# Transpositions of the normed x in the bank of the sums, in turn with the down products

## The chip, the cores and the metric

The kernel runs on one core of one Trainium2 chip. The metric is device time in microseconds of one execution: the median of several runs, here 661.32 us (three runs: 663.54, 661.32 and 660.82). Beside these stands one execution taken by the hardware profiler, from which all durations come.

## The reference

One transformer block in fp32 with the layer norm behind each residual sum, for x of shape 4 x 512 x 512 (batch, token, feature). The attention has 16 query heads of 32 and a single key and value head, with rotary positions; the feed-forward part has 1408 hidden units and ternary weights.

```python
q = rotary((x @ Wq + bq) heads); k = rotary(x @ Wk + bk); v = x @ Wv + bv
attn = softmax(q @ k.T / sqrt(32)); ctx = attn @ v
x = layernorm(x + ctx @ Wo + bo)
quantize(w) = clip(round(w / (mean(abs(w)) + 1e-8)), -1, 1)
hidden = sigmoid(x @ quantize(w1).T) * (x @ quantize(w2).T)
x = layernorm(x + hidden @ quantize(w3).T)
```

## The kernel before, in words

**Work and order.** The attention is cut into 64 steps (`steps`, L791): four batches b, four groups c of four heads, four tiles t of 128 keys. Step by step, `scores` (L414) writes the scores of one key tile for four heads into two double banks (PE, four products `ps` with the keys, then four that add minus the row maximum), ScalarE exponentiates them (`es`), and one step later `weigh` (L455) multiplies with v into `acc`. Each step also looks for the row maxima of a step seven ahead: `maximum` (L379) multiplies q and k again in the other orientation, one chunk of 128 queries at a time, and VectorE reduces each chunk (`maxima<-pmax`). The main loop (L865 on) issues chunk 0, then chunks 1 and 2 together, then chunk 3.

Everything else is filling between these pieces. `Fill` (L742) holds two lists of generators, `urgent` with the output projection of a batch (`project_out`, L588) and `gens` with the input projection and then `feed_forward` (L622), and takes from them in turn, one piece each, up to the microseconds due. A piece that yields 0 passes its turn to the other list. So while step n of batch b + 1 is computed, the output projection of batch b and the feed-forward part of batch b - 1 come to lie in between.

`project_out` ends with the part that is changed: for each of the four token tiles, four PE transpositions (`transpose`, L85) of the normed x into one bank `pt`, then `split` (L577): ScalarE copies the bank to a rounded y0, VectorE subtracts y0 from the bank to give y1 (`y<-pt,y`). Both halves, of all four tiles, are operands of the next batch's gate and up products (`gu`). `s.transposed` counts the tiles done.

`feed_forward` works in groups of hidden tiles. After the last group come the last down products: `po` for token tiles 0 and 1 together (twelve products), then for tile 2, then for tile 3 (six each). After each, VectorE adds half of `po` to x (`xt<-po,xt`, L700) and takes the statistics of the norm (`stats`, L560: `st`, `mv`). The loop at L681 holds these pieces back until the next batch has transposed enough tiles: two tiles before the first piece, three before the second, four before the third; after the last step (`now == len(steps)`) three, four and four.

**Banks.** The eight banks of the accumulator memory are split so: `ps_sc` has two double banks for scores and for maxima; `ps_acc` has one bank `acc` and one bank `den`; `ps_mm` has two single banks, taken in turn by every other product (`bank`, L226; in the tail every second one comes from `ps_sc`). `den` holds the sums of the exponentials in batch 0 (`count`, L464) and is the "bank of the sums" of the title. From batch 1 on POOL adds up the exponentials, and `den` serves for maxima: always that of chunk 0, and, once the last batch has been projected (`batches[-1].done == NC`), that of chunk 3 too (L385). A bank is free again when the engine that reads it has finished; whoever wants it next waits.

**What sets the order.** Each engine, and the queue of DMAs on SP, executes its instructions in the order in which the program issues them (`pin`, L67, forbids a reordering). PE, VectorE and ScalarE thus wait in line behind whatever stands ahead.

Of the kernel before, what the change touches and what calls it, by code (L numbers as in the profile page):

```python
# [10 lines left out]
F32 = mybir.dt.float32  # L11
# [9 lines left out]
P = 128  # L21
# [7 lines left out]
def postln_block(  # L29
# [16 lines left out]
    B, T, D = x.shape  # L46
    NC = D // P
    NT = T // P
    NF = wf.shape[1]
# [14 lines left out]
    ps_acc = ctx.enter_context(tc.tile_pool(name="ps_acc", bufs=1, space=PSUM))  # L64
# [14 lines left out]
    def mm(out, lhsT, rhs, start, stop):  # L79
        pin(nc.tensor.matmul(out, lhsT=lhsT, rhs=rhs, start=start, stop=stop))  # L80
# [36 lines left out]
    batches = [Batch() for _ in range(B)]  # L117

    chunks = iter([(b, c) for b in range(B) for c in range(NC)])
# [102 lines left out]

    swap = [(i + HALF) % HD for i in range(HD)]
    others = cycle((False, True))

    def bank(name):  # L226

        if now == len(steps) and next(others):
            return ps_sc.tile([P, 2, T], F32, tag="sc", name=name)[:, 0, :]
        return ps_mm.tile([P, T], F32, tag="mm", name=name)  # L230
# [133 lines left out]
    def room_for_maxima(b, c):  # L364

        return maxima[c % 2][:, 0 : NG * NT].rearrange("p (i t) -> p i t", t=NT)
# [12 lines left out]
    def maximum(b, c, i, chunks, q):  # L379


        s = batches[b]
        if i == 0 and chunks[0] == 0:
            s.mx[c] = room_for_maxima(b, c)
        if len(chunks) == 1 and (chunks[0] == 0 or batches[-1].done == NC):  # L385
            ps = ps_acc.tile([P, 1, T], F32, tag="den", name="pmax")
        else:
            ps = ps_sc.tile([P, 2, T], F32, tag="sc", name="pmax")
        ps = ps[:, 0 : len(chunks), :]
        for n, t in enumerate(chunks):  # L390
            mm(ps[:, n, :], q[:, ts(t, P)], s.kr, True, True)
        dve.tensor_reduce(s.mx[c][:, i, chunks[0] : chunks[-1] + 1], ps, AX.X, ALU.max)
# [195 lines left out]
    def project_out(b):  # L588

        s = batches[b]  # L590
        s.transposed = 0
        mv = small.tile([P, NT, 2], F32, tag="mv", name="mv")
        for t in range(NT):
            po = ps_mm.tile([P, D], F32, tag="mm", name="po")
            for c in range(NC):
                mm(po, s.ctxT[c][:, ts(t, P)], wo_sb[:, c, :], c == 0, c == NC - 1)
                if c == 1:
                    yield -1.8
            dve.tensor_tensor(s.x[t], s.x[t], po, ALU.add)
            stats(s.x[t], mv, t)  # L600
            if t == NT - 1:
                late.append((slot + 1, layernorm(s.x, mv)))
                ready = slot + 5
                s.projected = True
            yield 1.8

        while slot < ready or (b and not batches[b - 1].y_done):
            yield 0
        s.w = [load_weight(m, 0) for m in range(2)] + [load_weight(0, 1)]
        s.y = [work.tile([P, NC, T], F32R, tag=f"y{i}", name=f"y{i}", bufs=1) for i in range(2)]  # L610
        s.y_done = False
        for t in range(NT):
            pt = bank("pt").rearrange("p (c m) -> p c m", m=P)
            for c in range(NC):
                transpose(pt[:, c, :], s.x[t][:, ts(c, P)], ident)
            y = [half[:, :, ts(t, P)] for half in s.y]
            split(*y, pt)
            s.transposed = t + 1
            yield 0.9
        fill.add(feed_forward(b))  # L620

    def feed_forward(b):  # L622

        s = batches[b]
        mv = small.tile([P, NT, 2], F32, tag="mv2", name="mv2")
        after = [(m, f) for f in range(NF) for m in range(2)][3:]

        short = NF % 4 if b + 1 == B else 0
        ends = sorted({0, NF, *range(short, NF, 4)})
        parts = [range(*pair) for pair in zip(ends, ends[1:])]  # L630
        w3 = [[] for _ in parts]
        th = {}

        def product(k, m):
            w = s.w.pop(0).rearrange("p (c m) -> p c m", c=NC)
            if after:
                s.w.append(load_weight(*after.pop(0)))
            if len(w3[k]) < len(parts[k]):
                w3[k].append(load_weight(2, parts[k][len(w3[k])]))
            g = bank("gu")  # L640
            for c in range(NC):
                for i, part in enumerate(s.y):
                    mm(g, w[:, c, :], part[:, c, :], c == 0 and i == 0, c == NC - 1 and i == 1)
            return g

        def gate(k, f):

            th[f] = work.tile([P, T], F32, tag="th", name="th")
            act.activation(th[f], product(k, 0), AF.Tanh, scale=0.5)
            if b + 1 == B and f + 1 == NF:  # L650

                root = small.tile([P, 1], F32, tag="row", name="root")
                act.activation(root, eps_t, AF.Sqrt)

        for k, fs in enumerate(parts):
            h = []
            for f in fs:
                if f not in th:
                    gate(k, f)
                    yield 1.9  # L660
                up = product(k, 1)
                hw = work.tile([P, T], F32, tag="hw", name="hw")
                dve.scalar_tensor_tensor(hw, th[f], 1.0, up, ALU.add, ALU.mult)
                s.y_done = f == NF - 1
                h.append([hp.tile([P, T], F32R, tag="h", name=f"h{i}") for i in range(2)])

                if f == fs[-1]:
                    act.copy(h[-1][0], hw)
                yield 1.9
                if f < fs[-1]:  # L670
                    act.copy(h[-1][0], hw)
                dve.tensor_tensor(h[-1][1], hw, h[-1][0].bitcast(F32), ALU.subtract)
            if fs[-1] + 1 < NF:
                gate(k + 1, fs[-1] + 1)
                yield 1.9

            ahead = NT // 2 if fs[-1] + 1 == NF else 1
            for some in [range(ahead)] + [(t,) for t in range(ahead, NT)]:


                while fs[-1] + 1 == NF and b + 1 < B and 0 <= batches[b + 1].transposed <= min(  # L681
                    some[-1] + (now == len(steps)), NT - 1
                ):
                    yield 0
                pos = {t: bank("po") for t in some}
                last = len(fs) - 1
                early = [(t, n) for t in some for n in range(last)]

                put = len(early) - 1 if b + 1 == B and len(some) > 1 else len(early)
                for t, n in early[:put] + [(some[0], last)] + early[put:] + [(t, last) for t in some[1:]]:  # L690
                    for i in range(2):
                        mm(
                            pos[t],
                            h[n][i][:, ts(t, P)],
                            w3[k][n],
                            n == 0 and i == 0,
                            n == last and i == 1,
                        )
                for t in some:
                    dve.scalar_tensor_tensor(s.x[t], pos[t], 0.5, s.x[t], ALU.mult, ALU.add)  # L700
                    if fs[-1] + 1 < NF:
                        continue
                    stats(s.x[t], mv, t)
                    if b + 1 == B:
                        for done in range(max(t - 1, 0), t):
                            norm = layernorm(s.x[done : done + 1], mv[:, done : done + 1, :], True)
                            next(norm)
                            if t + 1 == NT:
                                end = last_scale(mv[:, t, :])
                            for _ in norm:  # L710
                                pass
                            late.append((slot + 1, store(b, done)))
                        if t + 1 == NT:
                            last_norm(s.x[t], *end)
                    elif t == NT - 1:
                        late.append((slot + 1, layernorm(s.x, mv)))
                yield 0.24 * 2 * len(fs) * len(some)
        if b + 1 < B:
            for t in range(NT):
                late.append((slot + 6, store(b, t)))  # L720
# [70 lines left out]
    steps = [(b, c, t) for b in range(B) for c in range(NC) for t in range(NT)]  # L791
# [6 lines left out]
    now = -1  # L798
# [66 lines left out]
    for n, (b, c, t) in enumerate(steps):  # L865
        now = n
# [46 lines left out]
    now = len(steps)  # L913
# [68 lines left out]
```

## Time and profile before

| | |
|---|---|
| median of the runs | 661.32 us |
| the profiled execution | 659.87 us, of which 658.1 us is its span |
| PE busy | 635.4 us, 3194 products |
| VectorE (DVE) busy | 440.3 us |
| ScalarE (ACT) busy | 282.6 us |
| GpSimd (POOL) busy | 327.4 us |
| granted PE clock, mean | 0.997 |
| 64 transpositions `pt<-ident,xt` | 272 ns each (median), from 227.0 to 587.6 us of the span |
| 16 copies `y<-pt` on ACT / 16 subtractions `y<-pt,y` on DVE | 586 ns / 681 ns each (median) |

The transpositions of batch 0 lie at 227 to 233 us of the span, those of batch 1 at 360 to 373, those of batch 2 at 495 to 509, and those of batch 3 after the last step, up to 588.

A row of the profile's groups reads: line and engine, operation, tile written <- tiles read (buffer numbers left out), shape, number of instructions | busy us, mean ns of one | idle us of the engine just before them, and which instruction ended most of that idle time. Nearly all PE work has line L80 and nearly all VectorE and ScalarE work L75, as small helpers issue them; so tiles are what to go by. A row of the timeline reads: start in the span, duration, engine, operation, and in brackets the idle time before it and what ended it. Neighbouring instructions of one kind are merged into one row, which then lasts from the first start to the last end. Ends of PE's products are modelled, and PE issues the next before the end of the last.

### The profile page before, as it was taken

Reading aid. Unit: us, or ns where it says so; the run is one execution under the profiler, and the core shown is the slowest. Engines: PE = TensorE matmul, PEld = TensorE weight load, DVE = VectorE, ACT = ScalarE, POOL = GpSimd, SP = SyncE. Lnnn points to the kernel's source line nnn. Section 1 sums busy time; section 2 is a strip of 40 time slices with the busy share of each in tenths; the row PEclk is TensorE's granted clock in tenths of the full one; section 3 lists DMA queues with packets and bytes.
Section 4 is the critical chain, followed back from the end, with each engine's and each line's share of the span. In section 5 each row is a group of like instructions: output and inputs, shape, how many; then the busy total and the mean of one; then the engine's idle time right before and its main releaser. Section 6 shows DMA issues by size and latency. Waiting matters only on the chain.

```text
span 658.1 us, 9358 instructions
## 1 busy us (share of the span) xinstructions
PE 635.4 (97%) x3194; PEld 357.2 (54%) x3194; DVE 440.3 (67%) x629; ACT 282.6 (43%) x441; POOL 327.4 (50%) x416
## 2 busy tenths in 40 slices
PE   8999999999999999999999899999998999999995
PEld 5233333443333356665555566655555685778884
DVE  3987765787998977676666867667536544364335
ACT  2474656564454645333244354333454521234213
POOL 2434344545998766467666275576575703202000
PEclk9999999999999999999999999999999999999998
DMA  8946669788676286464132457541131473237531
GB/s 265 316 164 209 204 194 273 230 254 259 171 238 205 89 250 190 136 191 147 46 106 77 117 163 219 158 143 44 55 116 52 145 236 120 81 112 229 175 109 64
DMA packets 60671, 107.78 MB, mean 164 GB/s; under 512 B 14592, under 2 KB 15360, under 8 KB 60624
## 3 DMA queue, kind: packets, MB, share of 16 engines
q1 hardware_dynamic: 51984, 80.57, 40.2%
q0 software_dynamic: 7920, 25.96, 12.3%
q10 hardware_dynamic: 720, 0.66, 0.4%
q8 instruction: 25, 0.41, 0.3%
q14 instruction: 22, 0.18, 0.1%
HBM read 84.06 MB, written 23.10 MB: 163 GB/s over the span
## 4 chain that ended last, share of the span: by engine, by line
PE 85%; DVE 9%; ACT 4%; issue 2%; POOL 0%; DVEq 0%; ACTq 0%; POOLq 0%
PE gu L80 24%; PE po L80 19%; PE ps L80 13%; PE pmax L80 9%; PE acc L80 7%; PE pq L80 7%; DVE maxima L75 3%; ACT es L75 2%; PE den L80 2%; PE pk L80 2%; DVE part L75 1%; DVE xt L75 1%; DVE y L75 1%; DVE st L75 1%; PE warm L80 1%
## 5 line engine op out<-in xcount | busy, mean ns | idle before, releaser
L75 DVE TENSOR_REDUCE maxima<-pmax 128x1 f32<-128x512 f32 (+1 forms) x169 | 157.8, 955 | 69.9 <-PE pmax L80 69.7
L75 ACT ACTIVATE es<-ps 128x1024 f32<-128x1024 f32 x128 | 124.2, 1021 | 117.6 <-PE ps L80 116.7
L80 PE MATMUL gu<-y,wg 128*128 128x512 f32 x704 | 171.6, 393 | 0.1
L80 PEld LDWEIGHTS gu<-y,wg 128*128 128x128 f32 x704 | 131.7, 188 | 33.7 <-issue 4.9
L75 POOL TENSOR_TENSOR total<-total,es 128x512 f32<-128x512 f32 x96 | 125.2, 1336 | 38.5 <-ACT es L75 38.3
L80 PE MATMUL po<-wd,h 128*128 128x512 f32 x352 | 86.5, 394 | 3.3 <-DVE y L75 2.9
L75 POOL TENSOR_TENSOR total<-es 128x512 f32<-128x512 f32 x48 | 60.9, 1302 | 52.5 <-ACT es L75 52.5
L80 PE MATMUL pmax<-kr,qr 128*128 128x512 f32 x192 | 74.7, 452 | 3.2 <-DVE maxima L75 1.0
L80 PEld LDWEIGHTS po<-wd,h 128*128 128x128 f32 x352 | 65.1, 188 | 20.8 <-DVE y L75 4.6
L75 ACT CAST h<-hw 128x512 fp32r<-128x512 f32 x44 | 27.3, 620 | 103.0 <-DVE hw L75 103.0
L80 PE MATMUL acc<-es,v 128*32 128x512 f32 x512 | 68.2, 605 | 0.0
L80 PEld LDWEIGHTS pmax<-kr,qr 128*128 128x128 f32 x192 | 34.6, 188 | 55.9 <-issue 17.0
L75 DVE SCALAR_TENSOR_TENSOR hw<-th,gu 128x512 f32<-128x512 f32 x44 | 30.2, 686 | 44.3 <-PE gu L80 43.1
L80 PE MATMUL po<-wo_sb,ctxT 128*128 128x512 f32 x128 | 58.8, 592 | 0.0
L75 DVE TENSOR_TENSOR h<-hw,h 128x512 fp32r<-128x512 f32 x44 | 44.2, 1005 | 21.7 <-ACT h L75 21.4
L80 PE MATMUL ps<-negm,ones_r 2*128 2x512 f32 x256 | 58.7, 788 | 0.0
L75 DVE SCALAR_TENSOR_TENSOR xt<-po,xt 128x512 f32<-128x512 f32 x48 | 32.8, 684 | 37.0 <-PE po L80 37.0
L80 PE MATMUL ps<-qT,kT 32*128 32x512 f32 x384 | 56.3, 640 | 0.0
L75 POOL DMA_DIRECT2D raw<-in_wf x66 | 36.0, 548 | 38.1 <-DMA w<-raw 27.2
L80 PE MATMUL pq<-xT,wq_sb 128*128 128x512 f32 x112 | 53.1, 602 | 0.9 <-ACT v L75 0.9
L75 ACT ACTIVATE th<-gu 128x512 f32<-128x512 f32 x44 | 26.3, 597 | 49.9 <-PE gu L80 49.8
L80 PEld LDWEIGHTS po<-wo_sb,ctxT 128*128 128x128 f32 x128 | 24.1, 189 | 21.2 <-issue 19.2
(99 smaller groups left out, 640.2 us busy)
## 6 DMA issues: line engine op xcount, KB each, us to landing
wg<-w SPq DMA_DIRECT2D x88, 256.0 KB
raw<-in_wf POOLq DMA_DIRECT2D x66, 256.0 KB, 4.6
qr<-qp SPq DMA_DIRECT2D x96, 128.0 KB
wd<-w SPq DMA_DIRECT2D x44, 256.0 KB
w<-raw POOLq DMA_DIRECT2D x33, 256.0 KB, 4.6
qp<-q SPq DMA_DIRECT2D x48, 128.0 KB
rden<-flat SPq DMA_DIRECT2D x64, 64.0 KB
xt<-in_x SPq DMA_DIRECT2D x16, 256.0 KB
```

Source lines behind the costliest of these rows:

```text
L75: return lambda *args, **kw: pin(getattr(self.engine, name)(*args, **kw))
L80: pin(nc.tensor.matmul(out, lhsT=lhsT, rhs=rhs, start=start, stop=stop))
```

## The change

Three things, all for the transpositions of batches 0, 1 and 2, and none after the last step:

- Their bank. Of batch 0, tiles 0 and 3 go into `den` and tiles 1 and 2 into `ps_mm`; of batches 1 and 2, tiles 0, 1 and 3 go into `den` and tile 2 into `ps_mm`.
- The maximum of chunk 3. In a step in which `den` has been given to a transposition (`turned`), it goes into a scores' bank in place of `den`.
- The turns. The first down piece (token tiles 0 and 1) waits for one transposed tile in place of two; the second and third wait as before. With the turns that `Fill` takes, the order for batches 1 and 2 is pt0, po0 and po1, pt1, pt2, po2, pt3, po3, where it was pt0, pt1, po0 and po1, pt2, po2, pt3, po3. For batch 0 there are no down products in between.

No instruction is added or taken away; the order on SP and POOL is unchanged, and so is that of VectorE and ScalarE for batch 0.

```diff
--- before.py
+++ after.py
@@ -222,6 +222,7 @@
 
     swap = [(i + HALF) % HD for i in range(HD)]
     others = cycle((False, True))
+    turned = [-1]
 
     def bank(name):
 
@@ -382,7 +383,7 @@
         s = batches[b]
         if i == 0 and chunks[0] == 0:
             s.mx[c] = room_for_maxima(b, c)
-        if len(chunks) == 1 and (chunks[0] == 0 or batches[-1].done == NC):
+        if len(chunks) == 1 and (chunks[0] == 0 or batches[-1].done == NC and turned[0] < now):
             ps = ps_acc.tile([P, 1, T], F32, tag="den", name="pmax")
         else:
             ps = ps_sc.tile([P, 2, T], F32, tag="sc", name="pmax")
@@ -610,7 +611,13 @@
         s.y = [work.tile([P, NC, T], F32R, tag=f"y{i}", name=f"y{i}", bufs=1) for i in range(2)]
         s.y_done = False
         for t in range(NT):
-            pt = bank("pt").rearrange("p (c m) -> p c m", m=P)
+            if now == len(steps) or (t in (1, 2) if b == 0 else t == 2):
+                pt = bank("pt")
+            else:
+
+                pt = ps_acc.tile([P, D], F32, tag="den", name="pt")
+                turned[0] = now
+            pt = pt.rearrange("p (c m) -> p c m", m=P)
             for c in range(NC):
                 transpose(pt[:, c, :], s.x[t][:, ts(c, P)], ident)
             y = [half[:, :, ts(t, P)] for half in s.y]
@@ -678,8 +685,8 @@
             for some in [range(ahead)] + [(t,) for t in range(ahead, NT)]:
 
 
-                while fs[-1] + 1 == NF and b + 1 < B and 0 <= batches[b + 1].transposed <= min(
-                    some[-1] + (now == len(steps)), NT - 1
+                while fs[-1] + 1 == NF and b + 1 < B and 0 <= batches[b + 1].transposed <= (
+                    min(some[-1] + 1, NT - 1) if now == len(steps) else some[-1] if len(some) == 1 else 0
                 ):
                     yield 0
                 pos = {t: bank("po") for t in some}
```

## The prediction

> **What bounds the kernel.** I read the page first: the busy shares, then the chain that ended last.
>
> ```profile
> span 658.1 us, 9358 instructions
> ...
> PE 635.4 (97%) x3194; PEld 357.2 (54%) x3194; DVE 440.3 (67%) x629; ACT 282.6 (43%) x441; POOL 327.4 (50%) x416
> ...
> PE 85%; DVE 9%; ACT 4%; issue 2%; POOL 0%; DVEq 0%; ACTq 0%; POOLq 0%
> ```
>
> TensorE (PE) is busy in 97% of the span, and 85% of the final chain is its work. Only about 22.7 us of PE idle exist in all, so the change can win only what is idle at the places it touches, and every microsecond of new PE idle is added to the time in full, because nothing later has slack to give it back. So the next view is PE's groups with the idle time just before them (instructions, busy us, mean ns | idle us and what ended it):
>
> ```profile
> L80 PE MATMUL po<-wd,h 128*128 128x512 f32 x352 | 86.5, 394 | 3.3 <-DVE y L75 2.9 <-DVE xt L75 0.3
> ...
> L86 PE MATMUL pt<-ident,xt 128*128 128x128 f32 x64 | 9.6, 278 | 3.7 <-DVE y L75 2.2 <-DVE q L75 1.1 <-DVE xt L75 0.3
> ```
>
> The transpositions (pt) and the down products (po) wait 7.0 us together, nearly all for a bank of `ps_mm` that VectorE (DVE) still reads. Where: the busy times by stretch (length, then PE, PEld, DVE, ACT, POOL busy, clock) of the three places where a batch's transpositions run inside the attention of a later batch:
>
> ```profile
> 226.00:235.00 9.00, 6.69 (x48) 3.02 (x40) 8.72 (x15) 5.32 (x8) 8.98 (x9) 1.00 0.82 243
> 358.00:374.00 16.00, 13.60 (x80) 8.26 (x78) 13.55 (x22) 5.39 (x9) 5.83 (x5) 1.00 0.46 133
> 495.00:511.00 16.00, 14.14 (x86) 8.06 (x86) 10.99 (x18) 6.54 (x9) 9.65 (x8) 1.00 0.17 52
> ```
>
> PE idles 2.31, 2.40 and 1.86 us there: 6.57 us is all that can be won (1.0%). The same lines warn: at the first two places DVE is busy 8.72 of 9 and 13.55 of 16 us. DVE's order is fixed, so whatever PE is made to wait for stands in a nearly full queue. The fourth batch's transpositions (from 575 us on) run after the last step, where the change keeps bank and order; they cost nothing new.
>
> **The change, place by place.** It adds and removes no instruction, and the queues of SP (DMA) and POOL keep their order. What changes is which bank each transposition has, hence what it waits for, and at the second and third place the order "pt0 pt1 | po0 po1 | pt2" becomes "pt0 | po0 po1 | pt1 pt2". From the built order of the changed kernel I took the instruction that each wait is for, and laid it on the times of this trace. Four durations recur, in us: `pt` x4 to the next PE instruction 0.36; one `po` product 0.25; scores' first `ps` to the first `acc` 1.30 (second pair of `ps` to `acc` 1.02); a single-chunk maximum on DVE 0.68.
>
> *First place.*
>
> ```profile
> 229.06 0.68 DVE L75 TENSOR_REDUCE maxima<-pmax 128x1 f32<-128x512 f32 x1
> 229.20 0.66 PE L86 MATMUL pt<-ident,xt 128*128 128x128 f32 x4 [1.13 <-DVE q L75]
> 232.13 0.66 PE L86 MATMUL pt<-ident,xt 128*128 128x128 f32 x4 [1.07 <-DVE y L75]
> 232.71 1.14 PE L80 MATMUL ps<-qT,kT 32*128 32x512 f32 x8
> ```
>
> Now pt0 runs at 227.01 in a free `ps_mm` bank. In the sums' bank (`den`) it must wait until DVE has reduced the maximum of chunk 0 that lies there, and DVE, still rotating q, starts that at 229.06: pt0 starts at 229.79. Queued behind pt0 on PE are two maxima products, the other transpositions and the scores; ScalarE (ACT) copies y at 230.5 (0.58), so DVE's first y starts at 231.10 instead of 229.7. The two later waits of pt (1.13 and 1.07) do go. But the maximum of chunk 3 has moved from `den` to the scores' banks, so the second pair of `ps` must wait for its reduction. DVE needs 3.01 from the first y to that reduction's end: 234.1. `acc` follows 1.02 later at 235.2; it was at 234.01. **+1.2 us.** Below: all 2.31 of idle go; above: pt0's whole delay of 2.78 (227.01 to 229.79) stays. I take the replay, as DVE is the full queue.
>
> *Second place.*
>
> ```profile
> 363.61 0.67 DVE L75 TENSOR_REDUCE maxima<-pmax 128x1 f32<-128x512 f32 x1
> 365.44 0.69 DVE L75 SCALAR_TENSOR_TENSOR xt<-po,xt 128x512 f32<-128x512 f32 x1 [1.15 <-PE po L80]
> 365.79 1.14 PE L80 MATMUL ps<-qT,kT 32*128 32x512 f32 x8
> 367.09 1.06 PE L80 MATMUL acc<-es,v 128*32 128x512 f32 x8
> 368.62 1.82 DVE L75 TENSOR_REDUCE maxima<-pmax 128x1 f32<-128x512 f32 x2
> 372.22 0.66 PE L86 MATMUL pt<-ident,xt 128*128 128x128 f32 x4 [1.11 <-DVE y L75]
> 373.63 0.66 DVE L75 TENSOR_REDUCE maxima<-pmax 128x1 f32<-128x512 f32 x1
> ```
>
> Here the down products no longer wait 0.98 and 0.31 for y; they wait for the last hidden chunk instead (DVE's h ends at 363.08, PE is there at 362.5), and PE reaches the scores at 364.25, 1.5 earlier. Then it stops. The product of chunk 3 now stands behind po0 and po1, so its reduction stands on DVE behind both additions into x and their statistics; and it lies in a scores' bank, so the second `ps` pair waits for it. DVE starts the first addition at 363.6 and needs 3.18 from there to the next reduction (365.44 to 368.62): the maximum runs 366.8 to 367.5, `ps` at 367.5, `acc` at 368.5 instead of 367.09: +1.4. Next step: maxima product of chunk 0 at 369.5, its reduction (PE to DVE 0.54, then 0.69) to 370.76, and only then pt1, as it is in `den`: 1.0 of PE idle. Then y1 (DVE 372.1), double maximum, the partial sum (1.23), y2, the third addition at 375.6 and, 1.54 behind that (372.09 to 373.63 in the trace), the reduction of chunk 3: 377.2 to 377.85. Again the second `ps` pair waits for it, where now it needs only ACT: `acc` at 378.9 instead of 374.11. **+4.8 us** together; ACT's exponentials, POOL's totals and later DVE work follow PE and have waits of their own to fill. SP's next load of heads waits for the moved product, 3 us later than now; behind it in SP's queue stands only the store of the partial sum, for which SP now waits 10.0 us. Below: −2.40 (all idle goes, the reductions are in time); above: the 3.18 of queue paid whole in both steps, +6.4.
>
> *Third place.*
>
> ```profile
> 501.12 2.11 PE L80 MATMUL po<-wd,h 128*128 128x512 f32 x8 [1.18 <-DVE y L75]
> 503.56 0.66 PE L86 MATMUL pt<-ident,xt 128*128 128x128 f32 x4 [0.33 <-DVE xt L75]
> 508.89 1.66 PE L80 MATMUL po<-wd,h 128*128 128x512 f32 x6 [0.35 <-DVE xt L75]
> ```
>
> All maxima are done, so `den` is really free. po0 and po1 start at 498.35 in banks freed long ago; pt2 is ready when the first addition ends (501.8); scores at 502.4 instead of 504.15; po3 needs y2 (505.4) and finds it done; the gate product ends up waiting 0.3 for the last y (508.6) and starts in effect at 508.4 instead of 510.41. **−2.0 us** (idle is counted from modelled matmul ends, so 1.86 of idle is 2.3 of lost issue). Below −2.3, above 0.
>
> **Sum.** +1.2 + 4.8 − 2.0 = +4.0. The profiled execution took 659.87 us (1.77 around its span): 663.9. The median of the runs shown is 661.32, which gives 665.3. I forecast **665.0**.
>
> **A rule that would make it worse.** In this trace PE never idles longer than 1.5 us, and the granted clock in all three stretches is 1.00; my replay has PE idle some 3.0 us (364.5 to 367.5) and 3.1 us (374.8 to 377.9). The Trainium skill, "TensorE: Matmul & The Clock Gate", section "What's actually happening", says that about 3.4 us of idle halve PE's clock until about 3.4 us of work have passed. No run here shows it yet; were a gap to count, an estimate from that page is 1.7 us more per gap, 668.4 for two.
>
> **Rivals.** *Faster:* the banks were the whole matter. Place: the scores' second `ps` pair at the second place. It decides from the point where the chunk-3 reductions end before PE gets there (by 364.5 and 374.7). Then that place gives up to −2.4, with the other two −3.2; if the first place's maximum also came in time, −6.57. Middle: 656.5. For it: the idle rows name exactly the banks that are changed. Against: the reductions would have to run 3 us earlier in a fixed queue. *No change:* only one of the two chunk-3 waits binds, because the trace's modelled PE ends hide some slack; 4.0 − 3.3 (the second wait's share, 4.8 − 1.4, nearly) = +0.7: 662.0. For it: DVE idles 1.15 just ahead of the first addition. *Worse:* both queues count whole (+6.4 at the second place) and the first place pays 2.78: +7.2, 668.5.
>
> **How the numbers follow.** Within 0.5% is 658.0 to 664.6, about what a measurement of this kernel can tell from no change. Forecast's case (+2.5 to +6, 663.8 to 667.3): 0.64, of which 0.09 falls within 0.5%; no change 0.22; worse 0.06; faster 0.08. So faster 0.08, same 0.31, slower 0.61. The range takes in the forecast's case and no change, and half a microsecond of run spread: 660.5 to 668.0.
>
> **What would show it.** Right: at about 227 us PE idle of some 2.5 before pt, ended by DVE maxima; about 365 and 376 us PE idle of 2.5 to 3 each before `ps`, ended by DVE maxima, a group that has no idle now; near 500 no idle before po. Wrong: no idle before `ps`, or the reductions of chunk 3 ahead of the additions on DVE. If `ps` waits but the time does not grow, my claim that PE has no slack later is wrong.

## The result and the profile after

The changed kernel takes 667.81 us (median of 6 runs, 667.32 to 670.95), the kernel before in the same runs 662.23 us (6 runs, 660.73 to 664.94). The ratio is 1.0089, with a 95% interval of 1.0069 to 1.0109: about 5.9 us slower, where I had forecast 3.7 us. The profiled execution took 667.70 us. The page of the changed kernel, read as before:

```profile
span 665.9 us, 9357 instructions
...
PE 641.1 (96%) x3194; PEld 360.4 (54%) x3194; DVE 439.0 (66%) x629; ACT 282.7 (42%) x441; POOL 328.0 (49%) x416
...
PEclk9999999999999999999999799999999999999998
...
PE 83%; DVE 8%; ACT 3%; DMA 2%; issue 2%; POOL 1%; SPq 0%; DVEq 0%; ACTq 0%; POOLq 0%
```

The span is 7.8 us longer with the same number of products. Idle time of PE grew by only 2.1 us (24.8 against 22.7); the other 5.7 us are *busy* time, 641.1 against 635.4. A part of that is only a way of counting: as the ends of products are modelled, the last products before a stop count as busy while PE already waits (at 367.45 below, four score products take 1.13 us; before the change eight took 1.14). For another part the clock strip names the reason: one slice of 40, at about 370 us, has a 7. The changed kernel's groups with the idle time before them:

```profile
L80 PE MATMUL po<-wd,h 128*128 128x512 f32 x352 | 87.0, 396 | 1.1 <-DVE h L75 0.7 <-DVE y L75 0.5
L80 PE MATMUL ps<-qT,kT 32*128 32x512 f32 x384 | 59.7, 640 | 3.6 <-DVE maxima L75 3.5
L86 PE MATMUL pt<-ident,xt 128*128 128x128 f32 x64 | 10.1, 294 | 3.4 <-DVE maxima L75 3.4
```

The down products' wait fell from 3.3 to 1.1 us, as the new banks were to do. The transpositions wait as long as before, but now for a maximum in `den`. And the scores, which had no such wait, lose 3.6 us to the maxima of DVE.

**First place** of the changed kernel, timeline:

```profile
229.74 0.68 DVE L75 TENSOR_REDUCE maxima<-pmax 128x1 f32<-128x512 f32 x1
230.48 0.66 PE L86 MATMUL pt<-ident,xt 128*128 128x128 f32 x4 [2.57 <-DVE maxima L75]
233.67 1.90 PE L80 MATMUL ps<-qT,kT 32*128 32x512 f32 x6 [0.47 <-DVE maxima L75]
236.16 1.06 PE L80 MATMUL acc<-es,v 128*32 128x512 f32 x8
```

The 2.57 before pt0 is the wait that I foresaw (2.5), and `acc` starts at 236.16 instead of 234.01 (0.73 of this is a lag from the start of the kernel, see below).

**Second place**, timeline (the changed kernel arrives here 3.15 us late):

```profile
366.87 0.69 DVE L75 SCALAR_TENSOR_TENSOR xt<-po,xt 128x512 f32<-128x512 f32 x1 [0.59 <-PE po L80]
367.45 1.13 PE L80 MATMUL ps<-qT,kT 32*128 32x512 f32 x4
369.94 0.66 DVE L75 TENSOR_REDUCE maxima<-pmax 128x1 f32<-128x512 f32 x1
370.65 0.70 PE L80 MATMUL ps<-qT,kT 32*128 32x512 f32 x2 [2.07 <-DVE maxima L75]
371.95 1.64 PE L80 MATMUL acc<-es,v 128*32 128x512 f32 x8
375.10 1.12 PE L86 MATMUL pt<-ident,xt 128*128 128x128 f32 x4 [0.78 <-DVE maxima L75]
377.57 2.35 PE L80 MATMUL po<-wd,h 128*128 128x512 f32 x6
381.88 0.66 DVE L75 TENSOR_REDUCE maxima<-pmax 128x1 f32<-128x512 f32 x1
382.60 0.70 PE L80 MATMUL ps<-qT,kT 32*128 32x512 f32 x2 [0.94 <-DVE maxima L75]
383.89 1.07 PE L80 MATMUL acc<-es,v 128*32 128x512 f32 x8
```

The first pair of scores (four rows of the trace) runs at 367.45, and then PE has nothing that it may do until DVE has reduced chunk 3 behind the two additions: the maximum ends at 370.60, the second pair starts at 370.65. The same comes back at 382.60. Now compare durations: eight `acc` take 1.64 us at 371.95 and 1.07 at 383.89; four `pt` take 1.12, where they took 0.66; six `po` take 2.35 (1.64 in a place with full clock). So for a part of the time between the two waits PE works at half its speed. The stretches, each 3.41 us (length, then PE, PEld, DVE, ACT, POOL busy, clock):

```profile
368.89:372.30 3.41, 1.65 (x12) 0.65 (x16) 1.64 (x4) 0.40 (x1) 0.00 (x0) 1.00 0.93 200
372.30:375.71 3.41, 2.63 (x12) 0.90 (x5) 0.69 (x1) 2.02 (x3) 0.00 (x0) 0.50 0.04 11
375.71:379.13 3.42, 3.42 (x13) 2.83 (x12) 2.26 (x3) 1.18 (x2) 0.00 (x0) 0.50 0.02 5
```

In the first, PE is busy for 1.65 of 3.41 us; in the next two the granted clock is 0.50. In the trace's record of the clock this is the only drop between the first microseconds and PE's last product: at 372.3 us, for 6.83 us. The trace of before has none in that time. (An estimate: PE's 6.05 us of work at half clock would take 3.0 us less at full clock, which is about half of the 5.7 us of added busy time.)

**Third place**, timeline:

```profile
508.15 3.14 PE L80 MATMUL po<-wd,h 128*128 128x512 f32 x12
511.13 1.14 PE L86 MATMUL pt<-ident,xt 128*128 128x128 f32 x8
512.19 1.14 PE L80 MATMUL ps<-qT,kT 32*128 32x512 f32 x8
```

No idle time stands before any of them: down products, transpositions and scores follow each other.

To see where the 7.8 us of span come from, I took the 512 `acc` products of both traces in their order, and noted how much later each starts:

| part of the span | growth of the lag, us |
|---|---|
| start, up to 52 us, where nothing is changed | +0.73 |
| first place (234 us), and a wait for weights in the next step | +1.41, +0.17 |
| a wait for weights at 300 us (0.58 before `gu`) | +0.84 |
| second place, first and second step (367 and 374 us) | +1.71, +4.92 |
| third place | −1.75, −0.22 |

The three places alone give 1.41 + 6.63 − 1.97 = +6.1 us, which agrees with the measured ratio (5.9). The rows at the start and at 300 us belong to this pair of executions: such shifts of 0.5 to 1 us come at several points in traces of several kernels below.

### The profile page after: what moved, and what is told of

Same layout as the page of the kernel before. It is cut to its first block, busy times and chain, and to the rows that moved or that the text cites. A ratio compares the mean times of both kernels' runs of the same rounds, so it can differ in the third digit from the quotient of the medians.

```text
span 665.9 us, 9357 instructions
## 1 busy us (share of the span) xinstructions
PE 641.1 (96%) x3194; PEld 360.4 (54%) x3194; DVE 439.0 (66%) x629; ACT 282.7 (42%) x441; POOL 328.0 (49%) x416
## 4 chain that ended last, share of the span: by engine, by line
PE 83%; DVE 8%; ACT 3%; DMA 2%; issue 2%; POOL 1%; SPq 0%; DVEq 0%; ACTq 0%; POOLq 0%
PE gu L80 23%; PE po L80 19%; PE ps L80 12%; PE pmax L80 9%; PE acc L80 7%; PE pq L80 7%; DVE maxima L75 3%; PE den L80 2%; ACT es L75 2%; PE pk L80 2%; DMA wg<-w 2%; DVE st L75 1%; DVE xt L75 1%; DVE part L75 1%; PE warm L80 1%
## 5 line engine op out<-in xcount | busy, mean ns | idle before, releaser
L80 PE MATMUL ps<-qT,kT 32*128 32x512 f32 x384 | 59.7, 640 | 3.6 <-DVE maxima L75 3.5
L80 PE MATMUL ps<-negm,ones_r 2*128 2x512 f32 x256 | 60.2, 780 | 0.0
L75 DVE TENSOR_TENSOR h<-hw,h 128x512 fp32r<-128x512 f32 x44 | 42.7, 971 | 21.8 <-ACT h L75 21.4
```

Source lines behind the costliest of these rows:

```text
L75: return lambda *args, **kw: pin(getattr(self.engine, name)(*args, **kw))
```

## Experiments

After the result I held this, called A in the expectations: the second place loses because chunk 3's maximum lies in a scores' bank while its reduction stands on DVE behind the additions that the new turns put ahead of it; a part of the loss is the halved clock that follows the stop; the third place gains for free. Rivals: the turns alone do it, the banks alone do it, or the clock is only a companion and costs nothing. Edits are against the changed kernel unless said otherwise.

**One place at a time.** `first_only`, `second_only` and `third_only` make the change for one batch (0, 1, 2) and leave the two others as before:

```diff
-            if now == len(steps) or (t in (1, 2) if b == 0 else t == 2):
+            if now == len(steps) or b not in (1,) or (t in (1, 2) if b == 0 else t == 2):
...
-                    ... else some[-1] if len(some) == 1 else 0
+                    ... else some[-1] if len(some) == 1 or b + 1 not in (1,) else 0
```

*First place alone.* 

> Only batch 0's transpositions get the new banks (and chunk 3 of that step moves); batches 1 and 2 keep the old banks and turns. My replay gave +1.2 us for this place and the two traces put it at +1.4, so: 1.2 to 1.6 us slower than before, ratio about 1.002, with PE idle about 2.5 us ahead of the first transposition, ended by the reduction of chunk 0. A rival, that PE's loss here is given back later because some later wait swallows it, expects no difference and a later wait of PE that is shorter by as much.

Measured: 662.66 us (12 runs), before 662.41 (29 runs), ratio 0.9999, 0.9978 to 1.0021. The trace shows the wait before pt0 (2.6 us) and +1.56 at the place, −0.40 in the next step: +1.2. In this trace the clock also halved at 231.1 us, for 3.41 us; the place itself costs only 0.15 us more than in the changed kernel's trace (+1.41), where it did not. An effect of 0.2% lies inside the interval, so the time decides nothing; the place's cost is read from the trace alone.

*Second place alone.* 

> Only batch 1's transpositions get the new banks and turns. Theory A (the scores wait for chunk 3's reduction, and the long idle of PE then also halves its clock for some microseconds): 6.0 to 6.8 us slower than before, ratio about 1.0095, with a granted clock near 0.5 in some 5 to 7 us after the first stop. Theory B (the waits alone, the lower clock of the changed kernel's trace being run to run chance): 4.8 us slower, ratio 1.007, clock 1.00 at that place.

Measured: 670.14 us (6 runs), ratio 1.0106, 1.0076 to 1.0137. In the trace the two steps cost +1.69 and +4.78, together +6.5, and the clock halves at 373.2 us for 6.83 us. The whole loss of the change, and more, is here.

*Third place alone.* 

> Only batch 2's transpositions get the new banks and turns. Theory: there no maxima are left to share the bank with, so the waits of the down products simply go: 2.0 us faster than before, ratio 0.997. Rival: what is won here is lost at the next product (weights not there, or the last y late): ratio 1.000.

Measured: 660.44 us (12 runs), ratio 0.9968, 0.9947 to 0.9989; the trace has −1.76 and −0.23 at the place. It gains, as forecast. The trace shows something else besides: at the first place, which this kernel leaves as before, the clock halved. Stretches, and then the timeline of `third_only`:

```profile
226.00:232.00 6.00, 4.08 (x25) 2.01 (x24) 5.93 (x10) 4.15 (x6) 5.98 (x8) 0.96 0.72 205
232.00:239.00 7.00, 6.64 (x28) 2.85 (x29) 3.95 (x8) 2.52 (x3) 5.31 (x5) 0.55 0.85 270
```

```profile
232.36 1.12 PE L86 MATMUL pt<-ident,xt 128*128 128x128 f32 x4 [1.07 <-DVE y L75]
233.41 2.09 PE L80 MATMUL ps<-qT,kT 32*128 32x512 f32 x8
```

Four transpositions take 1.12 us and eight scores 2.09, where the kernel before had 0.66 and 1.14 in its profile. The same order of work with the same wait (1.07 before pt) ran at full clock in one execution and at half in another. Here the lag to the kernel before grew by 2.3 us in this step and the next.

**The turns without the banks.** Every transposition back in `ps_mm`, chunk 3 back in `den`, the new turns kept:

```diff
-            if now == len(steps) or (t in (1, 2) if b == 0 else t == 2):
+            if True:
```

> The new turns for batches 1 and 2, but every transposition in the old pair of banks, so chunk 3's maximum stays in the bank of the sums. Theory A (the loss comes from chunk 3's maximum lying in a scores' bank while its reduction stands behind the additions): chunk 3 still stands behind the additions, but no scores wait for it; replayed, +0.7 us at the second place and -0.3 at the third, ratio 1.000 to 1.001, no PE idle ahead of the scores. Rival (the turns themselves are the loss, as the additions come ahead of the reduction on VectorE): 3 us slower or more, ratio 1.005 and above.

Measured: 661.64 us (12 runs), ratio 0.9996, 0.9974 to 1.0019; in the trace the second place costs −1.32 + 1.99 = +0.7, the third −0.2. Timeline of the second place:

```profile
365.64 1.14 PE L80 MATMUL ps<-qT,kT 32*128 32x512 f32 x8
366.94 1.06 PE L80 MATMUL acc<-es,v 128*32 128x512 f32 x8
368.14 0.66 DVE L75 TENSOR_REDUCE maxima<-pmax 128x1 f32<-128x512 f32 x1
368.85 0.50 PE L80 MATMUL pmax<-kr,qr 128*128 128x512 f32 x1 [0.85 <-DVE maxima L75]
```

Chunk 3's reduction is as late as in the changed kernel, at 368.14 behind the additions. But all eight scores have run 2.5 us before it, because its product lies in `den`; only the next maximum waits, for 0.85. A late reduction costs little in a bank that nobody on PE needs. So the turns alone are not the loss.

**The banks without the turns.**

```diff
-                while ... <= (min(some[-1] + 1, NT - 1) if now == len(steps) else some[-1] if len(some) == 1 else 0):
+                while ... <= min(some[-1] + (now == len(steps)), NT - 1):
```

> The new banks with the old turns (two tiles transposed ahead of the first down products). Theory A: at the second place chunk 3 of the first step stands ahead of the down products again, so its reduction is in time and the scores wait for nothing; what stays is a wait of the fourth transposition for a reduction of chunk 3 in the same bank: +0.4 and +2.1, so 2.5 us lost there, 1.5 at the first place, 1.5 to 2.0 won at the third: 2.3 us slower than before, ratio 1.0035. Rival (the banks alone carry the loss of the second place): 4.8 us or more there, ratio 1.007.

Measured: 666.20 us (8 runs), ratio 1.0051, 1.0028 to 1.0075. In the trace: first place +1.50 − 0.39, second 0.0 in the first step (A expected +0.4) and then +3.73 and +1.03, third −1.40 − 0.21. Timeline of the second place:

```profile
369.17 1.14 PE L80 MATMUL ps<-qT,kT 32*128 32x512 f32 x8
...
377.00 0.66 DVE L75 TENSOR_REDUCE maxima<-pmax 128x1 f32<-128x512 f32 x1
377.72 1.11 PE L86 MATMUL pt<-ident,xt 128*128 128x128 f32 x4 [3.23 <-DVE maxima L75]
381.21 1.94 PE L80 MATMUL acc<-es,v 128*32 128x512 f32 x8
```

With the old turns the first scores don't wait at all. The loss sits at pt3, which is in `den` and waits 3.23 us for a maximum. pt3 starts 2.13 us later than before (a replay of this order gives 2.1). The rest of the place, 2.6 us, I put down to the clock, half from 376.6 to 383.4 (eight `acc` in 1.94): the trace has no wait of PE there from pt3 to the end of the place, but no run with fillers tests this. So the banks alone lose too, by the other waits that they bring: the total of my rival, by the mechanism of A.

**The clock by itself.** Ten products without use in each of two steps (they write a scores' bank that the scores then overwrite) stand ahead of the scores at the second place, and fill the time in which PE otherwise stops for chunk 3:

```diff
+            if j == 0 and b == 2 and turned[0] == now - 1:
+                for _ in range(10):
+                    mm(ps[:, 0, :], ones_r, s.kr, True, True)
```

> The changed kernel with ten more products (ones by the keys, 128x512) ahead of the scores in the two steps in which the scores wait for chunk 3 at the second place; their results are overwritten by the scores. Ten products take about 2.5 us, less than each wait. Theory A (a stop of nearly 3 us lowers PE's clock, and that is the part that the replay lacked): the granted clock is 1.00 from 365 to 385 us, the second place costs 4.8 to 5.0 us instead of 6.6, and the kernel is 1.6 to 1.8 us faster than the changed one in spite of 20 more products: ratio to before 1.006. Theory B (the extra comes from the chain of waits, not from the clock): second place 6.6 or more, ratio 1.009 or above.

Measured: 664.91 us (12 runs), before 662.87 (24 runs), ratio 1.0048, 1.0027 to 1.0070. Stretches of `kept_busy` at the second place, then its timeline:

```profile
365.00:370.00 5.00, 5.00 (x28) 2.70 (x30) 3.20 (x7) 0.36 (x1) 0.80 (x1) 1.00 0.82 250
370.00:375.00 5.00, 4.22 (x27) 2.75 (x20) 2.42 (x3) 3.23 (x5) 0.00 (x0) 1.00 0.00 0
375.00:380.00 5.00, 4.94 (x27) 2.89 (x25) 4.93 (x9) 0.59 (x1) 0.00 (x0) 1.00 0.00 0
```

```profile
369.68 1.07 PE L80 MATMUL acc<-es,v 128*32 128x512 f32 x8
375.32 2.55 PE L80 MATMUL ps<-kr,ones_r 128*128 128x512 f32 x10
380.28 1.07 PE L80 MATMUL acc<-es,v 128*32 128x512 f32 x8
```

The clock is 1.00 in all three stretches, `acc` is back at 1.07, and the two steps cost +1.68 and +3.58 = +5.3 instead of +6.6. More work made the kernel faster: the first step is unchanged, and all of the difference, 1.4 us, is in the second, which is the step that ran at half clock. It is less than half of 6.83 us, as in this stretch PE also waits for others (0.78 before pt1, 0.94 before the second `ps` pair).

**The changed kernel again**, on the same chip as `kept_busy`, without an edit. 

> The changed kernel as it is, for a comparison on the same chip. Theory A: again a granted clock of 0.5 for 3.4 or 6.8 us after the first stop at the second place, 6.4 to 6.8 us lost there, ratio 1.009. If the lower clock were chance, it would lie elsewhere or be absent, and the second place would cost 4.8.

Measured: ratio 1.0069, 1.0043 to 1.0094, six runs of 665.30 to 668.91; a seventh execution, the profiled one, took 1578.77 us, has no record of the clock, and isn't read. So where the clock fell in these runs isn't shown; their mean clocks, 0.986 to 0.990, agree with a drop in each. The fillers of `kept_busy` are worth 0.2% by the ratios' middles, but the two intervals overlap: the clock's price is taken from the traces.

**A version that keeps what gains.** Batch 0 as before the change; of batch 1 only tile 1 in `den`, in the old turns, so that chunk 3 is reduced ahead of the additions; batch 2 as changed:

```diff
-            if now == len(steps) or (t in (1, 2) if b == 0 else t == 2):
+            if now == len(steps) or t not in ((), (1,), (0, 1, 3))[b]:
...
-                    ... else some[-1] if len(some) == 1 else 0
+                    ... else some[-1] if len(some) == 1 or b == 0 else 0
```

> Batch 2 as in the changed kernel; of batch 1 only the second tile goes into the bank of the sums, with the old turns; batch 0 as before. Theory A: -2.0 us at the third place as measured, and at the second the down products start 1.4 us earlier while chunk 3's reduction is still ahead of the additions: -1.1 us. Together 3.1 us faster than before, ratio 0.9953. Rival: moving chunk 3 to a scores' bank costs at any order, so the second place loses 1 us or more and the sum is -1 us or less, ratio 0.9985 or above.

Measured: 657.92 us (10 runs, 656.53 to 661.89), ratio 0.9935, 0.9912 to 0.9957. It beats both kernels. The trace has −1.45 at the second place and −1.76 − 0.24 = −2.00 at the third. Timeline and stretch of the second place in `mended`:

```profile
363.21 2.11 PE L80 MATMUL po<-wd,h 128*128 128x512 f32 x8 [0.24 <-DVE y L75]
364.59 0.67 DVE L75 TENSOR_REDUCE maxima<-pmax 128x1 f32<-128x512 f32 x1
365.25 1.13 PE L80 MATMUL ps<-qT,kT 32*128 32x512 f32 x6
366.62 1.07 PE L80 MATMUL acc<-es,v 128*32 128x512 f32 x8
```

```profile
358.00:374.00 16.00, 14.58 (x90) 9.30 (x90) 14.65 (x25) 6.39 (x10) 6.31 (x5) 1.00 0.43 133
```

Chunk 3 lies in a scores' bank here as well, but its reduction ends at 365.26, as PE reaches the scores, and costs nothing. PE is busy 14.58 of the 16 us, against 13.60 before the change.

**Fillers in the kernel before.** If the clock also falls by chance at the old first place, filling its two stops of 1.1 us should take away the longest runs. Against the kernel before:

```diff
+            if b == 0 and t in (1, 3):
+                if t == 1:
+                    idle = ps_sc.tile([P, 2, T], F32, tag="sc", name="idle")
+                for _ in range(4):
+                    mm(idle[:, t // 2, :], ones_r, batches[1].kr, True, True)
             pt = bank("pt").rearrange("p (c m) -> p c m", m=P)
```

> The kernel before, with eight more products (ones by the keys, 128x512, about 1 us for four) in the two stops of PE of 1.1 us each at the first place; their results are never read. Theory A (the runs of the kernel before spread because those stops let PE's clock fall in some executions, for one, two or more stretches of 3.4 us): the granted clock is 0.996 or more in nearly all runs, the slowest runs go, and the median falls from 662.4 to about 661, ratio 0.998. Theory B (the spread has another origin, and the stops are harmless): same spread, clocks down to 0.989 again, ratio 1.000.

Measured: 662.09 us (12 runs, 660.23 to 664.46), before 661.70 (19 runs, 659.69 to 665.24), ratio 1.0000, 0.9977 to 1.0023. The stops are filled. Timeline of `before_busy`:

```profile
231.10 0.66 PE L86 MATMUL pt<-ident,xt 128*128 128x128 f32 x4 [0.18 <-DVE q L75]
232.71 1.17 PE L80 MATMUL idle<-kr,ones_r 128*128 128x512 f32 x4
```

No run has a mean clock below 0.993, where 5 of the 19 runs of before have 0.989 to 0.992. But the median that I expected (661) did not come: the profiled execution of `before_busy` has its drop at 48.9 us, in the start-up, which the fillers don't reach. The theory fits the lowest clocks, though none of 12 against 5 of 19 can still be chance, and it failed for the median.

**Fillers in the mended kernel**, the same lines. 

> The same eight products in the kernel with the third place as changed and one tile of batch 1 in the bank of the sums. Theory A: medians 1 us below that kernel's 657.9, ratio to before 0.992, no run under a clock of 0.994. Theory B: as that kernel, ratio 0.9935.

Measured: 658.04 us (8 runs, 657.39 to 660.59), ratio 0.9941, 0.9919 to 0.9964: not faster than `mended`, so the microsecond that I expected was missed. Its trace shows shifts of +0.99, +0.79 and +0.47 us at 167, 240 and 300 us, where products wait for loads from memory (of x at the first, of weights at the two others). `second_only`, which has no fillers, has +0.63, +1.17 and +0.43 there, so the fillers need not be the cause.

## Why the forecast was right in its direction and too small

- **PE has no slack** (what bounds the kernel): held. The lag that each place adds is still there at the end of the span, and the places' sum, +6.1 us, is the measured 5.9.
- **First place, +1.2:** the trace shows +1.41 in the changed kernel and +1.2 in `first_only`. Both waits came as worked out (2.57 before pt0, and the second `ps` pair starts as chunk 3's reduction ends); the 0.2 that is missing is the time from that pair to `acc`, 1.30 (234.86 to 236.16) for my 1.02, as at the second place. The run times alone could not show an effect of this size.
- **Second place, +4.8: this is the step that failed, in size.** It measures 6.63 us. The waits are those of the replay: taking off the 3.15 us by which it arrives late, the second `ps` pair starts at 367.50, and I had 367.5. Two things were missing.
  - *The clock, 1.4 us.* I named the rule, set it beside the trace's clock of 1.00, and left it out of the sum: neither replayed stop (3.0 and 3.1 us) reached 3.4 us, and no run showed it. One drop came, at 372.3 us after the first of the two stops, and `kept_busy` shows its price: 6.63 − 5.26 = 1.4 us. Leaving it out was wrong. That the price lies near my 1.7 is luck: I had worked that out for 3.4 us of half clock, and the drop lasted 6.83, for which the same working gives 3.4.
  - *The time from the second `ps` pair to `acc`.* I took 1.02 us, from steps where that pair runs without a wait; behind a wait it is 1.30 (370.65 to 371.95) and 1.29 (382.60 to 383.89). Twice 0.27 is 0.5 us, which is about the rest: 5.26 − 4.8 = 0.46.
- **Third place, −2.0:** −1.97 in the changed kernel, −1.99 alone. The free bank, the early down products and the missing wait came as described.
- **Rivals.** *Faster* (the banks are the whole matter) fails: `banks_only` is slower, and the reductions did not come in time. Its condition was the right one, though: in `mended` the reduction ends as PE gets there, and that place gains. *No change* (only one of the two chunk-3 waits binds) fails by the rows at 370.65 and 382.60: both bind, though the idle times, 2.07 and 0.94 us, are smaller than my 2.5 to 3: the first is counted from a modelled end (from the start of the product before it, 2.66 us pass), and PE reached the second late, at half clock. *Worse* (668.5) had nearly the right total by other terms: it priced the first place at 2.78, which was not paid, and its +6.4 for the whole queue at the second place lies near the measured 6.63 by luck, as the clock made up the difference.
- **What is not settled.** The clock's effect in the times alone is not separated, as the intervals of `kept_busy` and `changed_again` overlap, and that the fillers keep the clock up rests on one trace. How often the drop at the second place comes isn't known, as two traces show it there (`second_only` the other) and the run times don't say where a clock fell. The waits for weights at 240 and 300 us come and go between executions, and no run here says what decides them. What the moved load of heads costs on its own was not tried.

## What to carry to other kernels

A bank that is read by an engine with a fixed, full queue binds its writer to the reader's place in that queue: before giving a tile another bank, look up what stands ahead of its reader, and who needs that bank next (the same late reduction cost 0.7 us in `den` and, with the banks moved, 5.3 in a scores' bank, without the clock). When a change opens a new stop on a matrix engine that has been kept busy, price the stop and, beside it, a stretch at half clock, and say how likely that is instead of leaving it out. Take a change at several places apart by place: this one loses 6.6 us at one and gains 2.0 at another, and the version that keeps the gain, and gives away a bank at the other only where its reduction comes in time, is 0.65% faster than the kernel before.

## What the runs showed of the hardware that I had not expected

**Half clock without an idle window.** In every trace where the clock fell between 48 and 380 us, it fell for 3.41 us or for 6.83 us, twice that, and to exactly half. Ten such drops lie in the traces; in the 3.41 us ahead of the seven shown here PE was busy for part of the time (the same holds for the three others: 1.22 us at 233.2 and 2.32 at 48.9 in `banks_only`, 2.31 at 48.9 in `second_only`):

| trace | drop at, us | PE busy in the 3.41 us before, us | at half clock, us |
|---|---|---|---|
| changed kernel | 372.3 | 1.65 | 6.83 |
| `second_only` | 373.2 | 1.76 | 6.83 |
| `banks_only` | 376.6 | 1.30 | 6.83 |
| `first_only` | 231.1 | 1.23 | 3.41 |
| `kept_busy` (first place) | 230.7 | 1.08 | 3.41 |
| `third_only` (place unchanged) | 231.5 | 1.99 | 6.83 |
| `before_busy` (start-up) | 48.9 | 2.33 | 3.41 |

The longest single stop of PE between its first and last product in any of these traces was 3.23 us (`banks_only`, of which 2.1 lay ahead of the drop); in `third_only` one of 1.11 us among transpositions lay ahead of it, and a second of 1.07 had only begun. The kernel before, in its own trace, had a stretch of 3.41 us with hardly more PE work (2.04 of 3.41 from 229.0 us on) and kept its clock.

How long a drop lasts goes with PE's work in it. In the six of 3.41 us PE was busy all through the drop; in the four of 6.83 us it was busy for only 2.28 to 2.63 of the first 3.41 us, and all through the second.

The Trainium skill, "TensorE: Matmul & The Clock Gate", section "What's actually happening", gives a window of 4096 cycles at 1.2 GHz, 3413 ns, that runs freely, and says that the clock is halved after at least one idle window. The lengths of 3.41 and 6.83 us agree with that window. That a window must be idle doesn't agree: with 1.1 to 2.3 us of work ahead of it the drop came all the same, if the record's times are the ends of windows, and with no stop over 3.23 us no window of 3.41 us can have been idle throughout. A window that runs freely would explain why the same place drops in one execution and not in another. The record of the clock supports it: within each trace all changes lie whole multiples of 3.413 us after the first, and that first change comes at 4.4 to 7.1 us of the span, as the execution has it. The three traces in which it comes earliest, at 4.4 to 4.6 us, are the three with the drop at 48.9 us; in the eight others (5.4 us or later) it is absent. How much work in a window is too little isn't found: cut at these multiples, `banks_only` has a window with 1.59 of 3.41 us busy (from 362.9 us) and no drop after it.

**The spread of the runs goes by the same steps.** Of the 72 runs of the kernel before that stand beside the experiments, 28 with a mean clock of 0.996 or more have a median of 660.83 us, 23 with 0.993 or 0.994 have 662.79, 7 with 0.991 or 0.992 have 663.19, and 14 with 0.988 to 0.990 have 664.81. A stretch of 3.41 us at half clock takes 3.41 / 2 / 658 = 0.0026 off the mean clock, so the three large groups lie between one and two stretches apart, and each step is worth some 2 us. The changed kernel, six runs with clocks of 0.983 to 0.993, is never in the uppermost group.
